# Routed experts' sums in the u buffers: more sets on the way, and the last x loaded beside the expert tiles

## The chip, the cores and the metric

The kernel runs on one core of a Trainium2 chip. The metric is the device time of one execution in microseconds (us), taken as the median of the runs shown. One further execution was taken with the hardware profiler on; all rows of profiles come from it.

## The reference

One decoder layer on x of shape (4, 512, 512) in f32: a selective state space block, a smooth-quantised gated linear block with weights that differ by batch, and a mixture of experts with top-2 routing over 16 experts and a shared expert. Each has a layernorm before it and a residual sum after it. The change is in the last part:

```python
routing = softmax(x @ gate_w.T)
topw, sel = top_k(routing, 2)
topw = topw / sum(topw)
hmid = silu(einsum('th,eih->tei', x, w1)) * einsum('th,eih->tei', x, w3)
moe_out = einsum('tei,ehi->th', hmid * combine[:, :, None], w2)   # combine: topw at sel
shared = sigmoid(x @ shared_gate_w.T) * (silu(x @ ws_gate.T) * (x @ ws_up.T) @ ws_down.T)
x = x + moe_out + shared
```

## The kernel before

The 2048 tokens are worked on in four batches of 512. Long scans over the state space fill the first 1450 us or so; behind them run, as Python generators, the back of each batch (`back`: output projection, quantised block, `moe_front` with the router and the shared expert) and the routed experts in two groups of two batches (`GROUPS`, `experts`). Group 0 is batches 0 and 1, group 1 is batches 2 and 3.

**Routed experts of a group.** `sort` puts the 1024 tokens x 2 choices in order of expert into 31 tiles of 128 rows; unused tiles have row numbers out of bounds, and their gathers move nothing. `expert_tiles` loads for each tile the tokens (`xs`, L1337, 256 KB) and the expert's weights (`wx`, L1146, 768 KB) by indirect DMA from POOL's queue. It then turns the tokens (PE L338, ACT L1357), multiplies (PE L1365), makes the gated product (ACT L1368, DVE L349 and L1371, tile `hs`), multiplies again (PE L1375), copies the result out (ACT L1378, `ys`, three buffers) and stores it to `y_d` in DRAM (SP, L1381). Up to three tiles are on their way at a time (`bank.depth`), and up to eight are loaded ahead (pool `last`, eight buffers).

**Sums of a group.** When the tiles are over, token block t (128 tokens, eight blocks to a group) has its sum made: x3 (residual plus shared expert) is loaded (SP, L1165), the two results of each token are gathered from `y_d` (POOL, L1168, two gathers), two DVE instructions add them with their weights into x (L1178), and SP stores the block to the output (L1185). I call what a block needs a set. `staged` writes the stages out as a software pipeline: in each step the later stages of earlier blocks come first, and an empty stage (`nothing`) puts one more set between load and add. Group 0 has its x in the tag `xs` and its two results in the tag `wx` of pool `experts`, with two buffers each; group 1 has them in the same tags of pool `last`, with eight.

**What sets the order of work.** Each engine, SP's and POOL's DMA queues among them, executes in the order in which the program was written. The class `Pace` carries a model of each engine's time and of the DMA queue (by tile name, it does not know that a buffer is used again), and the loop at the end of `run` (L1464) always advances the generator whose wait is over first in that model. So the model decides where on DVE a sum's add stands among the tiles' work. Group 0's sums start when group 1's first tiles have been loaded (`("begun", 1)`), group 1's when its tiles are over.

**The u buffers.** Pool `us` has 17 buffers of 128 x 512 f32. They hold `u`, the conv output of each batch (28 tiles in all go through them), until the batch's output projection is over; nothing uses them later.

Of the kernel before, what the change touches and what calls it, by code (L numbers as in the profile page):

```python
# [8 lines left out]
F32 = mybir.dt.float32  # L9
# [3 lines left out]
ALU = mybir.AluOpType  # L13
# [4 lines left out]
P = 128  # L18
B = 4
L = 512  # L20
DM = 512
# [39 lines left out]
class Bank:  # L61
# [21 lines left out]
    def staged(self, items, product, *stages, freed=1):  # L83

        gap = [nothing] * (self.depth - freed)
        return staged(items, product, *gap, *stages, every=1 if gap or self.depth == freed else freed, bank=self)
# [181 lines left out]
class Kernel:  # L268
# [860 lines left out]
    def experts(self, sb, group, bank, ahead):  # L1129


        nc = self.nc
        first, n = GROUPS[group]
        T, t0 = n * NT, first * NT
        NS = 2 * T + E - 1
        yield lambda: ("route", first + n - 1) in self.done
        place = lambda: (self.last, 8) if self.last else (sb, ahead)
        pos = sb.tile([P, T, 2], U32, name=f"pos{group}", bufs=1)
        tok = sb.tile([P, NS], U32, name=f"tok{group}", bufs=1)
        wrow = sb.tile([P, NS], U32, name=f"wrow{group}", bufs=1)  # L1140
        ws = {}

        def weights(s):

            ws[s] = place()[0].tile([P, W2 + DM], F32, name="wx")
            nc.gpsimd.indirect_dma_start(  # L1146
                out=ws[s],
                out_offset=None,
                in_=self.wexp,
                in_offset=bass.IndirectOffsetOnAxis(ap=wrow[:, s : s + 1], axis=0),  # L1150
                bounds_check=E * P - 1,
                oob_is_err=False,
            )

        yield from self.sort(sb, bank, group, pos, tok, wrow, lambda: [weights(s) for s in range(ahead)], min(ahead, 3))
        y_d = self.dram.tile([NS * P, DM], F32, name=f"y_d{group}")
        yield from self.expert_tiles(group, place, bank, NS, tok, ws, weights, self.xn_d[group], y_d)
        self.done.add(("tiles", group))

        yield lambda: ("moe", first + n - 1) in self.done and ("begun", len(GROUPS) - 1) in self.done  # L1160
        xr, ys = {}, {}

        def load(t):
            xr[t] = sb.tile([P, DM], F32, name="xr4", tag="xs")
            nc.sync.dma_start(xr[t], self.x3[t0 + t])  # L1165
            ys[t] = sb.tile([P, 2, DM], F32, name="yg", tag="wx")
            for i in range(2):
                nc.gpsimd.indirect_dma_start(  # L1168
                    out=ys[t][:, i, :],
                    out_offset=None,  # L1170
                    in_=y_d,
                    in_offset=bass.IndirectOffsetOnAxis(ap=pos[:, t, i : i + 1], axis=0),
                )
            return ys[t], xr[t]

        def add(t):
            for i in range(2):
                nc.vector.scalar_tensor_tensor(  # L1178
                    xr[t], ys[t][:, i, :], self.topw[:, t0 + t, i : i + 1], xr[t], ALU.mult, ALU.add
                )  # L1180
            return xr[t]

        def store(t):
            b, r = divmod(t0 + t, NT)
            nc.sync.dma_start(self.out[b, r * P : (r + 1) * P, :], xr[t])  # L1185

        yield from staged(range(T), load, *[nothing] * (ahead - 2), add, store)

    def sort(self, sb, G, group, pos, tok, wrow, first_weights, few):

# [136 lines left out]
        G.done(pk)  # L1327
        yield

    def expert_tiles(self, group, place, bank, NS, tok, ws, weights, xn_d, y_d):  # L1330

        nc = self.nc
        xs, rows = {}, xn_d.shape[0]

        def load(s):
            xs[s] = place()[0].tile([P, DM], F32, name="xs")
            nc.gpsimd.indirect_dma_start(  # L1337
                out=xs[s],
                out_offset=None,
                in_=xn_d,  # L1340
                in_offset=bass.IndirectOffsetOnAxis(ap=tok[:, s : s + 1], axis=0),
                bounds_check=rows - 1,
                oob_is_err=False,
            )
            if s not in ws:
                weights(s)

        def steps(s):

            sb, ahead = place()  # L1350
            few = min(ahead, 3)
            yield PE, xs[s], bank.free
            tp = bank.take([P, NK, P])
            self.transposes(tp, xs[s], NK)
            yield ACT, tp
            xT = sb.tile([P, NK, P], F32, name="xT", bufs=few)
            nc.scalar.copy(xT, tp)  # L1357
            bank.done(tp)
            w = ws[s]
            yield PE, xT, w, bank.free  # L1360
            ph = bank.take([P, 2, P])
            for i in range(2):
                for k in range(NK):
                    o = (2 * k + i) * P
                    nc.tensor.matmul(ph[:, i, :], w[:, o : o + P], xT[:, k, :], start=(k == 0), stop=(k == NK - 1))  # L1365
            yield ACT, ph
            h = sb.tile([P, P], F32, name="hs", bufs=few)
            nc.scalar.activation(h, ph[:, 0, :], AF.Tanh, scale=0.5)  # L1368
            yield h
            self.swish(h, h, ph[:, 0, :])  # L1370
            nc.vector.scalar_tensor_tensor(h, h, 0.5, ph[:, 1, :], ALU.mult, ALU.mult)  # L1371
            bank.done(ph)
            yield PE, h, bank.free
            py = bank.take([P, DM])
            nc.tensor.matmul(py, h, w[:, W2:], start=True, stop=True)  # L1375
            yield ACT, py
            y = sb.tile([P, DM], F32, name="ys", bufs=few)
            nc.scalar.copy(y, py)  # L1378
            bank.done(py)
            yield SP, y  # L1380
            nc.sync.dma_start(y_d[s * P : (s + 1) * P, :], y)  # L1381

        going = []
        loaded = started = ended = 0
        while ended < NS:
            while loaded < NS and loaded - ended < place()[1]:
                load(loaded)
                loaded += 1
            self.done.add(("begun", group))
            while started < loaded and len(going) < bank.depth:  # L1390
                going.append(Steps(self.pace, steps(started)))
                started += 1
            self.pace.update()
            one = min(going, key=lambda g: self.pace.ready(g.wait))
            yield one.wait
            one.go()
            if one.over:
                going.remove(one)
                ended += 1
# [231 lines left out]
```

## Time and profile before

| | us |
|---|---|
| median of 3 runs | 1704.43 (1701.28 to 1705.39) |
| profiled execution: time | 1707.47 |
| profiled execution: span | 1705.8 |
| last y_d store issued | 1673.9 |
| group 0's sums: first gather, last add | 1530.3, 1603.8 |
| group 1's sums: first gather, last add | 1676.7, 1702.1 |

How to read the lines below. PE is the matmul engine, PEld its weight load, DVE the vector engine, ACT the scalar engine, POOL GpSimd, SP the sync engine (its queue is SPq). A group of instructions shows line, engine, operation, output <- inputs, shapes, count | busy us, mean ns | idle us of that engine just before, and what ended most of it. A stage table has start:end, length, busy us of each engine with its number of instructions in brackets, the granted TensorE clock as a share of full speed, the busy share of the 16 DMA engines, and GB/s. Lines of the timeline have start, length, engine, line, operation, and in square brackets the idle time before it with what ended it.

### The profile page before, as it was taken

What the parts mean: (1) busy time and instruction counts of PE and PEld (TensorE: products, weight loads), DVE (VectorE), ACT (ScalarE), POOL (GpSimd) and SP (SyncE); (2) the same over time, 40 slices, a digit from 0 to 9 for tenths busy, and PEclk for the clock granted to TensorE, in tenths of its full rate; (3) what the DMA queues carried; (4) which work ended last, traced back from release to release, by engine and by line L of the source; (5) the groups of instructions that cost most, each with busy time, mean ns of one, the idle gap of its engine ahead of it and who ended that gap; (6) DMA issues with size and microseconds to landing.
All of it is one profiled execution on the core that took longest, in us unless ns stands there. A gap on an engine that the chain in (4) does not pass through costs nothing. (4 is left out here: it accounts for less than half of the span.)

```text
span 1705.8 us, 16157 instructions
## 1 busy us (share of the span) xinstructions
PE 1270.8 (75%) x4916; PEld 641.2 (38%) x4924; DVE 1230.2 (72%) x1367; ACT 912.4 (53%) x1490; POOL 1127.5 (66%) x911
## 2 busy tenths in 40 slices
PE   6768577659666687997669848766568989788891
PEld 2222122113332243434234314434243467545681
DVE  3286999997998798898889978888897643443213
ACT  3365677654778765556876522777653136401340
POOL 1175999886888797777879654788785532153443
PEclk9978689759798788999888978878878999789896
DMA  3464455574554465764456572546574653367846
GB/s 104 105 156 111 93 134 118 115 196 86 128 110 100 96 178 140 179 170 110 92 122 165 132 217 57 151 121 154 152 218 140 240 192 107 129 254 235 336 137 221
DMA packets 108310, 255.89 MB, mean 150 GB/s; under 512 B 16192, under 2 KB 20416, under 8 KB 108224
## 3 DMA queue, kind: packets, MB, share of 16 engines
q1 hardware_dynamic: 91776, 198.21, 45.1%
q0 software_dynamic: 16448, 56.65, 9.6%
q8 instruction: 39, 0.64, 0.2%
q14 instruction: 47, 0.39, 0.1%
HBM read 158.59 MB, written 45.88 MB: 120 GB/s over the span
## 5 line engine op out<-in xcount | busy, mean ns | idle before, releaser
L634 POOL TENSOR_TENSOR bu<-bc,rep 128x1024 f32<-128x1024 f32 x256 | 602.7, 2359 | 186.5 <-DVE da L641 155.8
L641 DVE TENSOR_TENSOR_SCAN da<-da,bu 128x1024 f32<-128x1024 f32 x256 | 585.9, 2289 | 73.3 <-POOL bu L634 52.7
L632 ACT ACTIVATE da<-rep,a_sb 128x512 f32<-128x512 f32 x512 | 353.0, 691 | 313.1 <-DVE h L647 288.6
L647 DVE TENSOR_TENSOR h<-da,bc 128x1024 f32<-128x1024 f32 x256 | 312.3, 1220 | 25.8 <-PE py L659 15.3
L659 PE MATMUL py<-h,sel 128*32 128x512 f32 x1024 | 168.7, 680 | 59.3 <-DVE h L647 59.3
L1146 POOL DMA_INDIRECT wx<-in_wexp,wrow x62 | 63.3, 1021 | 82.3 <-PE bank L1375 32.8
L392 PE MATMUL bank_a<-xnT,win 128*128 128x512 f32 x192 | 99.3, 665 | 15.3 <-DVE gz L349 8.3
L448 POOL TENSOR_TENSOR u<-u,tap 128x511 f32<-128x511 f32 (+2 forms) x72 | 91.3, 1268 | 16.4 <-ACT tap L444 14.1
L659 PEld LDWEIGHTS py<-h,sel 128*32 128x32 f32 x1024 | 30.6, 117 | 177.0 <-DVE h L647 93.9
L392 PE MATMUL bank_g<-xnT,win 128*128 128x512 f32 x168 | 83.4, 642 | 3.2 <-DVE gz L349 2.1
L603 POOL TENSOR_TENSOR sp_e<-sp_e,dd 128x512 f32<-128x512 f32 x32 | 40.6, 1270 | 62.7 <-ACT dd L598 62.7
L1337 POOL DMA_INDIRECT xs<-xn_d,tok x62 | 63.9, 1030 | 19.4 <-issue 13.7
L392 PE MATMUL bank_b<-xnT,win 128*128 128x512 f32 x120 | 62.7, 671 | 18.1 <-ACT sp_r L592 16.4
L392 PEld LDWEIGHTS bank_a<-xnT,win 128*128 128x128 f32 x192 | 40.2, 216 | 73.0 <-issue 52.0
L1168 POOL DMA_INDIRECT yg<-y_d,pos x32 | 32.2, 1005 | 48.9 <-DMA y_d<-ys 25.5
L1365 PE MATMUL bank<-xT,wx 128*128 128x128 f32 x448 | 55.4, 282 | 1.0 <-ACT xT L1357 1.0
L327 POOL TENSOR_SCALAR ln_scale<-ln_mv 128x1 f32<-128x1 f32 x48 | 11.1, 231 | 67.8 <-DVE ln_mv L320 64.6
L1178 DVE SCALAR_TENSOR_TENSOR xr<-yg,topw,xr 128x512 f32<-128x512 f32 x32 | 23.8, 754 | 43.2 <-DMA xr<-x 23.7
L1365 PEld LDWEIGHTS bank<-xT,wx 128*128 128x128 f32 x448 | 53.6, 197 | 3.4 <-issue 1.4
L711 PE MATMUL bank_a<-wout,u 128*128 128x512 f32 x92 | 45.4, 650 | 11.7 <-DMA wout<-in_wout 6.1
L392 PEld LDWEIGHTS bank_g<-xnT,win 128*128 128x128 f32 x168 | 33.3, 205 | 52.2 <-issue 43.7
L655 PE MATMUL py<-u,skip 128*128 128x512 f32 x64 | 37.8, 676 | 10.8 <-DVE u L681 10.8
(407 smaller groups left out, 2490.6 us busy)
## 6 DMA issues: line engine op xcount, KB each, us to landing
rep<-dd SPq DMA_DIRECT2D x128, 512.0 KB, 8.2
win<-in_win SPq DMA_DIRECT2D x64, 256.0 KB, 3.0
y_d<-ys SPq DMA_DIRECT2D x62, 256.0 KB, 2.5
x<-xr SPq DMA_DIRECT2D x48, 256.0 KB, 2.1
xr<-x SPq DMA_DIRECT2D x48, 256.0 KB, 4.4
bc<-rows_d SPq DMA_DIRECT2D x32, 256.0 KB, 5.4
gz_d<-gz SPq DMA_DIRECT2D x32, 256.0 KB, 3.0
gzl<-gz_d SPq DMA_DIRECT2D x32, 256.0 KB, 4.5
```

Source lines behind the costliest of these rows:

```text
L392: nc.tensor.matmul(pj, win[:, k, :], xnT[:, k, :], start=(k == 0), stop=(k == NK - 1))
L448: nc.gpsimd.tensor_add(u[:, j:], u[:, j:], v[j][:, j:])
L603: nc.gpsimd.tensor_sub(e, e, du)
L632: nc.scalar.activation(da[:, i, :], rep[:, i, 0, :], AF.Exp, scale=self.a_sb[:, q, g : g + 1])
L634: nc.gpsimd.tensor_mul(bu, st["bc"][0, g].unsqueeze(1).to_broadcast([P, NP, L]), rep[:, :, 1, :])
L641: self.nc.vector.tensor_tensor_scan(daf, daf, buf, 0.0, ALU.mult, ALU.add)
L647: self.nc.vector.tensor_mul(h, st["da"].pop((c, n)), st["bc"][1, g].unsqueeze(1).to_broadcast([P, NP, L]))
L659: nc.tensor.matmul(py[q * CH : (q + 1) * CH, :], self.sel, st["h"][c, g, q // NP][:, q % NP, :], start=False, stop=(g == NG - 1),)
L711: nc.tensor.matmul(po[t], st["u"][c][:, t * P : (t + 1) * P], wout[:, c, :], start=(c == part[0]), stop=(c == part[-1]),)
L1146: nc.gpsimd.indirect_dma_start(out=ws[s], out_offset=None, in_=self.wexp, in_offset=bass.IndirectOffsetOnAxis(ap=wrow[:, s : s + 1], axis= ...
L1337: nc.gpsimd.indirect_dma_start(out=xs[s], out_offset=None, in_=xn_d, in_offset=bass.IndirectOffsetOnAxis(ap=tok[:, s : s + 1], axis=0), bo ...
L1365: nc.tensor.matmul(ph[:, i, :], w[:, o : o + P], xT[:, k, :], start=(k == 0), stop=(k == NK - 1))
```

## The change

Group 0's sums take their x and their two results from the pool `us`, in tiles of one buffer each, so that three buffers make a set; and there are three empty stages instead of none, so that five sets are on the way. Group 1 keeps its results in pool `last` with six empty stages as before, but has its x in `us`. A new function `some`, called by `expert_tiles` when all 31 tiles' loads are written, loads the eight x of group 1's sums there, provided that group 0's sums and the last `moe_front` are already written.

```diff
+        xr = {}
+
+        def fetch(t):
+            xr[t] = self.us.tile([P, DM], F32, name="xr4", tag="u")
+            nc.sync.dma_start(xr[t], self.x3[t0 + t])
+
+        def some():
+
+            if sb is self.last and not xr and {("sums", 0), ("moe", B - 1)} <= self.done:
+                for t in range(T):
+                    fetch(t)
+
+        yield from self.expert_tiles(group, place, bank, NS, tok, ws, weights, some, self.xn_d[group], y_d)
...
         def load(t):
-            xr[t] = sb.tile([P, DM], F32, name="xr4", tag="xs")
-            nc.sync.dma_start(xr[t], self.x3[t0 + t])
-            ys[t] = sb.tile([P, 2, DM], F32, name="yg", tag="wx")
+            if t not in xr:
+                fetch(t)
+            if sb is self.last:
+                both = sb.tile([P, 2, DM], F32, name="yg", tag="wx")
+                ys[t] = [both[:, i, :] for i in range(2)]
+            else:
+                ys[t] = [self.us.tile([P, DM], F32, name="yg", tag="u") for i in range(2)]
...
-        yield from staged(range(T), load, *[nothing] * (ahead - 2), add, store)
+        yield from staged(range(T), load, *[nothing] * (6 if sb is self.last else 3), add, store)
+        self.done.add(("sums", group))
...
             self.done.add(("begun", group))
+            if loaded == NS:
+                some()
```

More of the change, by code (lines that the diff above doesn't have):

```diff
@@ L1156, in experts @@
         y_d = self.dram.tile([NS * P, DM], F32, name=f"y_d{group}")
-        yield from self.expert_tiles(group, place, bank, NS, tok, ws, weights, self.xn_d[group], y_d)
+        xr = {}
[7 more added lines that the diff above has]
+        yield from self.expert_tiles(group, place, bank, NS, tok, ws, weights, some, self.xn_d[group], y_d)
         self.done.add(("tiles", group))
         yield lambda: ("moe", first + n - 1) in self.done and ("begun", len(GROUPS) - 1) in self.done
-        xr, ys = {}, {}
+        ys = {}
         def load(t):
-            xr[t] = sb.tile([P, DM], F32, name="xr4", tag="xs")
-            nc.sync.dma_start(xr[t], self.x3[t0 + t])
-            ys[t] = sb.tile([P, 2, DM], F32, name="yg", tag="wx")
+            if t not in xr:
[5 more added lines that the diff above has]
+                ys[t] = [self.us.tile([P, DM], F32, name="yg", tag="u") for i in range(2)]
             for i in range(2):
                 nc.gpsimd.indirect_dma_start(
-                    out=ys[t][:, i, :],
+                    out=ys[t][i],
                     out_offset=None,
@@ L1173, in load @@
                 )
-            return ys[t], xr[t]
+            return *ys[t], xr[t]
         def add(t):
@@ L1178, in add @@
                 nc.vector.scalar_tensor_tensor(
-                    xr[t], ys[t][:, i, :], self.topw[:, t0 + t, i : i + 1], xr[t], ALU.mult, ALU.add
+                    xr[t], ys[t][i], self.topw[:, t0 + t, i : i + 1], xr[t], ALU.mult, ALU.add
                 )
@@ L1328, in sort, with expert_tiles @@
         yield
-    def expert_tiles(self, group, place, bank, NS, tok, ws, weights, xn_d, y_d):
+    def expert_tiles(self, group, place, bank, NS, tok, ws, weights, some, xn_d, y_d):
         nc = self.nc
```

## The prediction

> **What bounds the kernel now.** First the page: no engine is full over the span, so the edited stage has to be read by itself: adds of 754 ns that sat idle 43.2 us, 23.7 of them for x. The edited code runs only after about 1490 us.
>
> ```profile
> span 1705.8 us, 16157 instructions
> ...
> L1178 DVE SCALAR_TENSOR_TENSOR xr<-yg,topw,xr 128x512 f32<-128x512 f32 x32 | 23.8, 754 | 43.2 <-DMA xr<-x 23.7
> ```
>
> Next the stage table of the tail, cut at the starts of the transposes of each three tiles of group 1 (the bank depth is three). Columns: stretch, length, busy time of PE, PEld, DVE, ACT, POOL, granted clock, DMA share, GB/s.
>
> ```profile
> 1564.40:1583.00 18.60, 12.24 (x67) 8.75 (x66) 3.71 (x9) 3.57 (x8) 8.49 (x10) 0.75 0.86 313
> 1583.00:1592.78 9.78, 9.78 (x68) 8.19 (x67) 3.11 (x8) 4.16 (x9) 6.60 (x7) 0.96 0.98 365
> 1592.78:1607.07 14.29, 10.55 (x67) 8.00 (x66) 3.14 (x8) 3.47 (x8) 8.76 (x9) 0.90 1.03 410
> 1607.07:1620.60 13.53, 12.57 (x67) 10.69 (x66) 1.73 (x6) 4.65 (x10) 3.21 (x4) 0.72 0.72 292
> 1620.60:1630.01 9.41, 9.41 (x67) 7.79 (x66) 1.73 (x6) 4.06 (x9) 5.98 (x6) 1.00 0.87 279
> ```
>
> The last row is a round of three tiles bound by TensorE at full clock: 9.41 us, as are all later ones to tile 30. Tiles 4 to 15 took 18.60+9.78+14.29+13.53 = 56.2 us where four such rounds are 37.6: 18.6 us are lost here. The chain of waits says to what.
>
> ```profile
> 1560.48 6.90 DMA out<-xr
> 1567.40 8.09 DMA xr<-x
> 1575.61 0.76 DVE xr L1178
> ...
> 1577.72 5.50 PE bank L1375 x6
> ...
> 1584.32 10.40 DMA out<-xr
> 1594.73 8.17 DMA xr<-x
> 1603.03 0.76 DVE xr L1178
> ```
>
> The sums of group 0 have two x buffers. SP waits until a store of out has left one (6.90 us), only then loads x into it (8.09), and the add waiting for it stands on DVE ahead of the hs of tiles 4 to 6. PE then idles 6.36 us, and runs six L1375 matmuls in 5.5 us that take 2.74 in a warm round: the granted clock of that stage is 0.75. The same again before tile 12. In the list of waits from 1530 to 1610, that is (total us, times, longest)
>
> ```profile
> DVE xr L1178 <- DMA xr<-x: 23.7, 4, 10.3
> ...
> ACT ys L1378 <- DMA y_d<-ys: 8.4, 3, 4.9
> ...
> PE bank L1375 <- DVE hs L1371: 6.4, 1, 6.4
> ```
>
> and on SP's own queue (engine, line, what it waited for; us in total, times, longest)
>
> ```profile
> SPq L1165 <- DMA out<-xr: 31.1, 6, 9.7
> ```
>
> The end, last: POOL issues the 16 gathers of group 1 when the last y_d has landed.
>
> ```profile
> 1674.39 3.70 SPq L1165 DMA_DIRECT2D xr<-x  x8
> 1676.67 0.96 POOL L1168 DMA_INDIRECT yg<-y_d,pos  x1 [25.52 <-DMA y_d<-ys]
> ...
> 1697.09 0.95 POOL L1168 DMA_INDIRECT yg<-y_d,pos  x1 [0.30 <-issue]
> ...
> 1702.07 0.75 DVE L1178 SCALAR_TENSOR_TENSOR xr<-yg,topw,xr 128x512 f32<-128x512 f32 x1 [1.12 <-DMA yg<-y_d,pos]
> ```
>
> **The change, part by part.** No instruction is added: 16 x loads, 32 gathers, 32 adds, 16 stores as before. Their buffers and places move.
>
> *Five sets of group 0 on the way.* Sets 0 to 3 are loaded at once, set t+4 with the add of t. 28 tiles u have gone through the 17 buffers, so set t takes allocations 28+3t to 30+3t, and each waits for the one 17 before it. Sets 0 to 4 replace u's whose out_proj is long over: no wait. On SP two more x loads go ahead of L999 at 1491 (2 x 0.41 us): those land at 1496 and serve an add at 1551.73, so nothing. x4 follows at about 1495, x5 to x7 each directly behind the issue (no longer the landing) of the store of set 0, 1, 2, by the old add times 1541, 1545, 1554. On POOL, the gathers of sets 2 and 3 move up behind 1535.0 (4 x 1.26 us, to 1540), set 4 to about 1543; old times 1541 to 1555. They pass no tile gather: the ninth xs (1556.70) comes after, and wx of tile 9 waits for PE until 1559.69 anyway. DMA has room: the loads and outs that leave the crowd after 1559 are yg of sets 5 to 7 (1.57 MB), some x and outs, together 2.4 MB by my count; between 1540 and 1560 the share was 0.59.
>
> *A wait added.* The second gather of set 5, 6, 7 gets the buffer of x0, x1, x2, and so waits on POOL for the landing of that set's store. With adds 0 to 2 at about 1539, 1543, 1552 and 2 to 4 us for a store here, that is until 1545, 1548, 1557. Behind it on POOL stands the xs of tile 9, at most 2 us late; its weights are wanted at about 1575 and land 8.9 us after issue, so a hold is free until 1566. Before, POOL waited 12.9 us for adds in the same place.
>
> *What DVE then sees.* The adds wait only for loads four steps old: set 7 lands at about 1562, its add falls at about 1565. The adds (12 us in all) move ahead of tile 7, among the shared expert's DVE work of 1540 to 1567, where DVE is half idle. So the four waits of 23.7 us go, with both PE stalls and the cold rounds after them.
>
> *What is late next.* DMA. A round loads and stores 3 x (786+262+262) KB = 3.93 MB; the busiest stage above moved 410 GB/s, so 9.6 us. y_d landed after 8 to 11.6 us in the crowd, and only three ys buffers stand between ACT and it: a round shorter than the landing plus 0.7 us makes ACT wait (the 8.4 us above). I give each of the four rounds 0.7 us for this, 40.5 us in all, and 1.5 us for the two rounds of tiles 16 to 21, which become crowded. Gain 56.2 - 40.5 - 1.5 = 14.2 us; bounds 18.6 (no crowd) and 0 (see the rivals).
>
> Here a rule speaks against the change. The Trainium skill, "DMA: Bandwidth & Descriptors", section "Where 436 GB/s comes from", says that transfers between HBM and SBUF are held to some 358 GB/s per core. By the rule a round is 3.93 MB / 358 = 11.0 us, six rounds 66 instead of 62, and the gain about 10. The stage row with 410 (14 us long) is over the rule; I take the row.
>
> *x of the last sums.* Eight SP issues (3.7 us) move from 1674.4 to about the time when tile 24 is over, between y_d stores of a stage with a DMA share of 0.26 (rounds of tiles 25 to 30); their buffers are those of group 0's sets 2 to 4, free by then. SP is idle there, a y_d store slips by at most 3.7 us, ys has three buffers, nothing. At the end 2.1 MB (5 to 6 us of DMA) leave a stretch that POOL sets: 16 gathers at the usual 1.255 us start within 18.8 us, they took 20.4 (some 1.39 to 1.46 us each). I take this 1.6 us, and 0.6 of the last landing (5.0 us, against 3.7 in the lighter 1530 to 1559), 2.2 in all; bounds 0 and 4.
>
> **Sum.** 14.2 + 2.2 = 16.4 us of the profiled 1707.5 (span 1705.8) gives 1691; the profiled run is 3 us over the median 1704.4, so against that 1688.
>
> **The rivals.**
> *The crowd keeps the time (A).* With the stall gone TensorE asks for weights sooner, y_d lands after 11.6 us as in 1590 to 1600, and rounds are 12.3 us: six of them 74, against 56.2+18.8 = 75 before. Only the end's 2 us is left: 1702. For it: DMA shares of 0.98 and 1.03 now. Against: those rounds also carried group 0's sums, and the round at 0.98 took only 9.78. A half-way form, rounds of 11, gives 1694.
> *POOL held by the store's landing (B), the slower one.* If a store of set 0 to 2 stands on SP behind a y_d or x3 store that waits, the gather of set 5 to 7 holds POOL, and with it xs and wx of tile 9 on. From 1566 each us of hold is a us of PE; it must last to about 1582 to eat the gain and to 1590 to reach 1711. For it: SP is in order, and a store of out took up to 14.8 us to land. Against: the y_d stores start only at 1560, and adds 0 to 2 have nothing late before them.
> *The change doesn't bite (C).* If the written order still puts adds before their data, DVE waits as before, for the gathers: half of the 23.7 us stays, the gain is 7 + 2: 1695.
>
> **How the numbers follow.** Forecast 0.58 (1688, 1681 to 1693), half-way A and C 0.22 (1693 to 1699), full A 0.08 (1700 to 1705), B 0.12 (1710 to 1716). 0.3% is 5 us, about what a measurement of this kernel can tell from no change. Below 1699.3: 0.80; within: 0.08; above 1709.5: 0.12, as B when it acts is seldom small. The range goes from 1680 (both upper bounds, 22.6 us, and a us or two of noise) to 1702, leaving out B and some of A.
>
> **What would show it.** Right: no DVE wait for x at L1178 before 1650, SP's wait on out gone, tiles 4 to 15 in 38 to 43 us at a clock near 1.0, all adds of group 0 before about 1570, eight x loads among the y_d stores before 1660, 16 last gathers within 19 us. Wrong: a wait of POOL for out over 8 us, ACT ys waits for y_d over 2 us a round, PE idle behind wx, or DVE waiting for yg in front of an hs.

## The result, and the profile after

The changed kernel takes 1691.13 us (median of 7 runs, 1685.40 to 1695.48), the kernel before, beside it, 1704.22 us. The ratio is 0.9923, 95% interval 0.9905 to 0.9941: 13.1 us faster. (Beside the later experiments the kernel before has medians of 1703.55 to 1704.52 us; each ratio is to the runs beside it.) The forecast was 1688, with a range of 1680 to 1702. A repeat on another chip gave 1689.97 us and a ratio of 0.9924 (0.9901 to 0.9948).

The page of the profiled execution (1690.85 us) has this span. Lines in the changed kernel are numbered higher: the add L1178 is L1194, the x load L1165 is L1161, the store L1185 is L1201, the gather L1168 is L1184, and the tile lines L1365, L1375, L1381 are L1382, L1392, L1398.

```profile
span 1689.1 us, 16148 instructions
```

The stage table, cut as before at the first transposes of each three tiles (the last three columns are PE's clock, the share of the DMA engines and GB/s): tiles 4 to 21, and tiles 28 to 30 in the last row.

```profile
1563.30:1572.67 9.37, 9.37 (x67) 7.79 (x66) 2.47 (x7) 3.57 (x8) 3.50 (x4) 1.00 1.00 394
1572.67:1582.08 9.41, 9.41 (x68) 7.79 (x66) 1.72 (x6) 4.06 (x9) 5.97 (x6) 1.00 1.01 386
1582.08:1591.49 9.41, 9.41 (x67) 7.79 (x66) 1.72 (x6) 4.06 (x9) 4.98 (x5) 1.00 1.02 379
1591.49:1602.14 10.65, 9.52 (x68) 7.79 (x66) 1.72 (x6) 4.06 (x9) 6.98 (x7) 1.00 1.02 395
1602.14:1611.55 9.41, 9.41 (x68) 7.79 (x66) 1.72 (x6) 4.06 (x9) 5.97 (x6) 1.00 0.95 365
1611.55:1621.65 10.10, 9.51 (x68) 7.79 (x67) 1.72 (x6) 4.06 (x9) 5.98 (x6) 1.00 0.27 83
...
1640.47:1651.19 10.72, 9.51 (x68) 7.79 (x67) 1.73 (x6) 4.06 (x9) 0.00 (x0) 1.00 0.21 79
```

Four rounds that took 18.60, 9.78, 14.29 and 13.53 us now take 9.37, 9.41, 9.41 and 10.65, with the clock at 1.00 throughout, though the DMA engines are full for the first 38 us of it. PE is the bound in three of the four rounds, with no idle time, and DMA just keeps up.

The timeline of DVE shows where group 0's adds went. All sixteen are over at about 1560, with no idle time before any of them (a bracket would stand at the end of the line), and the hs of tiles 4 on waits for ACT alone:

```profile
1542.43 2.98 DVE L1194 SCALAR_TENSOR_TENSOR xr<-yg,topw,xr 128x512 f32<-128x512 f32 x4
...
1558.28 1.53 DVE L1194 SCALAR_TENSOR_TENSOR xr<-yg,topw,xr 128x512 f32<-128x512 f32 x2
...
1567.03 0.29 DVE L349 SCALAR_TENSOR_TENSOR hs<-hs,bank_g 128x128 f32<-128x128 f32 x1 [2.78 <-ACT hs L1385]
```

In the list of POOL's waits from 1500 on, a gather waits once for an older set's buffer, and it waits for an add, not for a store to land (total, times and longest in us):

```profile
POOL yg L1184 <- DVE xr L1194: 0.9, 1, 0.9
```

In the list of all engines from 1560 to 1660, two of ACT's waits at its copies into ys:

```profile
ACT ys L1395 <- PE bank_b L338: 1.5, 1, 1.5
...
ACT ys L1395 <- DMA y_d<-ys: 1.0, 1, 1.0
```

The second of these is in the round of 10.10 us. The first, in the round of 10.65 us, is put down to PE, but ACT's other copies of the kind waited 0.6 us for PE; that this one too waited for a ys buffer is an inference that the kernel with ys in u, below, tests. A third such wait is in the round of tiles 28 to 30, behind the eight early x loads, and it too is put down to PE (timelines of SP and of ACT):

```profile
1631.77 3.67 SPq L1161 DMA_DIRECT2D xr<-x  x8
1635.54 22.22 SPq L1398 DMA_DIRECT2D y_d<-ys  x8
...
1642.02 0.59 ACT L1395 COPY ys<-bank 128x512 f32<-128x512 f32 x1 [1.58 <-PE bank_a L338]
```

The end stage did not become shorter. The last y_d store is issued at 1657.44 and the span ends at 1689.1: 31.7 us, against 31.9 before. In the timeline of its POOL and DVE:

```profile
1660.20 0.95 POOL L1184 DMA_INDIRECT yg<-y_d,pos  x1 [26.83 <-DMA y_d<-ys]
...
1663.58 0.75 DVE L1194 SCALAR_TENSOR_TENSOR xr<-yg,topw,xr 128x512 f32<-128x512 f32 x1 [8.02 <-DMA yg<-y_d,pos]
1663.97 1.18 POOL L1184 DMA_INDIRECT yg<-y_d,pos  x1 [0.30 <-issue]
...
1668.12 0.75 DVE L1194 SCALAR_TENSOR_TENSOR xr<-yg,topw,xr 128x512 f32<-128x512 f32 x1 [0.93 <-DMA yg<-y_d,pos]
1668.32 1.37 POOL L1184 DMA_INDIRECT yg<-y_d,pos  x1 [0.30 <-issue]
1669.99 0.94 POOL L1184 DMA_INDIRECT yg<-y_d,pos  x1 [0.30 <-issue]
1670.01 0.75 DVE L1194 SCALAR_TENSOR_TENSOR xr<-yg,topw,xr 128x512 f32<-128x512 f32 x1 [1.13 <-DMA yg<-y_d,pos]
...
1680.88 1.47 POOL L1184 DMA_INDIRECT yg<-y_d,pos  x1 [0.30 <-issue]
```

The gathers are still spread over 20.7 us (1660.20 to 1680.88), and seven of the sixteen take 1.07 to 1.47 us instead of 0.95. Each of those seven starts at least 0.10 us into an add; the one at 1669.99 starts just before its add and is not slow, and one that starts 0.03 us into an add (1671.24) is not slow either. That became a theory of its own, below.

**How the later tables are made.** The long scans are the same in all kernels, and still tile 4 starts up to 7 us apart from one profiled execution to the next. So profiles are compared from the tail's own marks: the rounds of three tiles, from the transposes of tile 4 to the issue of the last y_d store ("tiles"), and from there to the end of the span ("end"). Before: tiles 109.5, end 31.9. After: tiles 94.1, end 31.7. Each is one execution. A second one of the changed kernel has 93.8 and 32.2, so its stages repeat within about half a us. Those of kernels that stall can differ more: the kernel with early x only, below, leaves group 0's sums as they were, and its tiles take 107.1 where the kernel before has 109.5.

### The profile page after: what moved, and what is told of

Its sections match the earlier page's. It is cut to its first block, busy times and chain, and to the rows that moved or that the text cites. A ratio compares the mean times of both kernels' runs of the same rounds, so it can differ in the third digit from the quotient of the medians.

```text
span 1689.1 us, 16148 instructions
## 1 busy us (share of the span) xinstructions
PE 1271.8 (75%) x4924; PEld 640.6 (38%) x4924; DVE 1229.9 (73%) x1367; ACT 912.7 (54%) x1490; POOL 1129.1 (67%) x911
## 5 line engine op out<-in xcount | busy, mean ns | idle before, releaser
L659 PE MATMUL py<-h,sel 128*32 128x512 f32 x1024 | 173.1, 701 | 55.1 <-DVE h L647 55.0
L659 PEld LDWEIGHTS py<-h,sel 128*32 128x32 f32 x1024 | 31.9, 120 | 176.4 <-DVE h L647 90.0
L1354 POOL DMA_INDIRECT xs<-xn_d,tok x62 | 64.0, 1032 | 19.4 <-issue 13.1
L1184 POOL DMA_INDIRECT yg<-y_d,pos x32 | 33.3, 1042 | 36.8 <-DMA y_d<-ys 26.8
L327 POOL TENSOR_SCALAR ln_scale<-ln_mv 128x1 f32<-128x1 f32 x48 | 11.1, 230 | 67.4 <-DVE ln_mv L320 64.2
L1382 PE MATMUL bank<-xT,wx 128*128 128x128 f32 x448 | 53.6, 276 | 1.7 <-ACT xT L1374 1.7
L1382 PEld LDWEIGHTS bank<-xT,wx 128*128 128x128 f32 x448 | 51.8, 192 | 4.2 <-ACT xT L1374 2.2
L349 DVE SCALAR_TENSOR_TENSOR hs<-hs,bank 128x128 f32<-128x128 f32 x28 | 8.0, 285 | 53.9 <-ACT hs L1385 53.9
```

The source lines that it names most:

```text
L659: nc.tensor.matmul(py[q * CH : (q + 1) * CH, :], self.sel, st["h"][c, g, q // NP][:, q % NP, :], start=False, stop=(g == NG - 1),)
L1354: nc.gpsimd.indirect_dma_start(out=xs[s], out_offset=None, in_=xn_d, in_offset=bass.IndirectOffsetOnAxis(ap=tok[:, s : s + 1], axis=0), bo ...
```

## The experiments

Theory 1 was that of the prediction: group 0's adds stood on DVE waiting for x, which waited on SP for a buffer. What had to be told apart was the buffer from the lead (how early a set is loaded), and this half of the change from the other (x of the last sums loaded early).

| kernel | ratio to before (95%) | tiles us | rounds of tiles 4-6, 7-9, ... 28-30 | end us |
|---|---|---|---|---|
| before | 1 | 109.5 | 18.60 9.78 14.29 13.53 9.41 9.41 9.41 9.41 9.41 | 31.9 |
| changed | 0.9923 (0.9905 to 0.9941) | 94.1 | 9.37 9.41 9.41 10.65 9.41 10.10 9.41 9.41 10.72 | 31.7 |
| changed, once more | 0.9924 (0.9901 to 0.9948) | 93.8 | 9.37 9.41 9.41 9.87 9.57 10.34 9.41 9.41 10.74 | 32.2 |
| five sets, late x | 0.9914 (0.9889 to 0.9938) | 92.7 | 9.37 9.41 9.41 9.80 9.62 10.63 9.41 9.41 9.41 | 32.1 |
| early x only | 1.0013 (1.0002 to 1.0024) | 107.1 | 16.05 11.38 14.53 9.86 10.12 9.41 9.41 9.41 10.72 | 32.2 |
| two sets in u | 0.9958 (0.9938 to 0.9977) | 97.8 | 9.47 9.41 13.47 9.41 9.41 10.53 9.41 9.41 11.02 | 31.4 |
| only group 0's x in u | 0.9950 (0.9930 to 0.9970) | 98.8 | 9.79 10.24 11.16 10.68 13.00 9.41 9.41 9.41 9.41 | 31.0 |
| changed, x in PSUM at the end | 0.9931 (0.9913 to 0.9948) | 94.3 | 9.37 9.41 9.41 10.65 9.40 9.81 9.41 9.41 11.22 | 30.3 |
| changed, x one by one | 0.9923 (0.9905 to 0.9941) | 93.0 | 9.37 9.41 9.41 11.05 9.41 9.88 9.41 9.41 9.41 | 32.7 |
| changed, ys in u | 0.9901 (0.9882 to 0.9920) | 90.9 | 9.38 9.41 9.40 9.38 9.37 9.38 9.37 9.37 9.65 | 32.1 |
| all three | 0.9894 (0.9876 to 0.9913) | 90.6 | 9.37 9.41 9.41 9.37 9.37 9.38 9.37 9.37 9.38 | 29.8 |

### One half of the change and the other

The changed kernel without the early x:

```diff
-            if loaded == NS:
-                some()
```

> The changed kernel without `some`: group 0 with five sets in u buffers, but the last sums' eight x are loaded at the end, behind the last y_d store, as before. Theory 1 (all of the gain is the wait of group 0's adds for x that is gone; the end stage took 31.9 us before and 31.7 after): as the changed kernel, 1690 to 1693 us, and an end stage of 31 to 33 us from the issue of the last y_d store. Rival (the early x saves the predicted 2 us at the end, hidden in the spread): 1693 or more, an end stage of 33.5 us or more.

1686.38 us, a little under what was expected. All of the gain is there; the end is 32.1 us, not 33.5, and the round of tiles 28 to 30, 10.72 us with early x, is at 9.41. So the second half brings nothing, and costs 1.3 us in that round of the profile. The ratio is lower than that of the changed kernel (0.9914 against 0.9923), but the intervals overlap, so the times alone do not show the loss.

The other half alone (group 0 as before, the last x early). The cut is against the kernel before; `fetch`, `some` and its call are added as in the change:

```diff
...
-            xr[t] = sb.tile([P, DM], F32, name="xr4", tag="xs")
-            nc.sync.dma_start(xr[t], self.x3[t0 + t])
+            if t not in xr:
+                xr[t] = sb.tile([P, DM], F32, name="xr4", tag="xs")
+                nc.sync.dma_start(xr[t], self.x3[t0 + t])
...
```

> The second half alone: the last sums' x in u buffers and loaded beside the tiles; group 0's sums with two sets and their old buffers. Theory 1: no gain, 1703 to 1705 us, with the DVE waits for x of 20 us or more as before. Rival (early x is worth the predicted 2 us): 1701 to 1702.5 us.

1705.78 us: no gain, if anything a loss (ratio 1.0013, interval above 1). In the list of waits DVE still waits for x:

```profile
DVE xr L1192 <- DMA xr<-x: 23.6, 4, 10.8
```

The slow round of 10.72 us at the end of the tiles is there too, so it goes with the early x. The profiled execution was one of this kernel's faster ones: its tail is 2.0 us shorter than that of the kernel before, and the medians say otherwise. Its rounds of tiles 4 to 15 take 51.8 us where the kernel before has 56.2, with the same stall in them; a difference of this size between single profiles of such kernels tells nothing.

### The buffer or the lead

The changed kernel with two sets of group 0 on the way:

```diff
-        yield from staged(range(T), load, *[nothing] * (6 if sb is self.last else 3), add, store)
+        yield from staged(range(T), load, *[nothing] * (6 if sb is self.last else 0), add, store)
```

> The changed kernel with no empty stage for group 0: two sets on the way as before, but each in fresh u buffers, so that neither x nor results wait for an older set to leave. Theory 1a (the reuse of a buffer is what cost): most of the gain stays, 1691 to 1695 us, DVE waits at the adds under 5 us. Theory 1b (the lead of a set is what counts: x of set t+1 is still issued on SP behind the store of set t-1, and lands late in the crowd): half or less of the gain, 1697 to 1703 us, DVE still waits 10 us or more at the adds.

1694.97 us, just over half of the gain in time; in the profile 11.7 of the 15.4 us of tiles (109.5 to 97.8). Neither expectation holds as it stood: the time is in the range of 1a, the waits of DVE at the adds are 6.1 us (3.8 for yg, 2.3 for x) where 1a had under 5 and 1b 10 or more, and PE hardly feels them (the round of tiles 4 to 6 takes 9.47 us). What is left is the one round of 13.47 us, and its lines in the timeline of ACT and PE name another cause:

```profile
1577.77 0.59 ACT L1395 COPY ys<-bank 128x512 f32<-128x512 f32 x1 [1.60 <-DMA y_d<-ys]
...
1579.73 0.58 ACT L1395 COPY ys<-bank 128x512 f32<-128x512 f32 x1 [1.37 <-DMA y_d<-ys]
...
1580.85 3.68 PE L1382 MATMUL bank_b<-xT,wx 128*128 128x128 f32 x16 [2.33 <-ACT xT L1374]
```

ACT waits twice for a ys buffer to reach DRAM, the next xT stands behind that, PE idles 2.33 us and runs 16 matmuls in 3.68 us (granted clock 0.54) where a round at full clock has 1.95. 2.33 and 1.73 are the 4.06 us that the round lost. So the lead matters, but through ys, not through a wait at an add: the three y_d stores of tiles 4 to 6, whose buffers these copies need, took 8.5 to 11.1 us to land here, and 4.5 to 7.8 in the changed kernel. In this kernel the last set's two gathers and x load, and the last three stores of out, fall between 1554 and 1565, among the tiles' weights; with five sets the gathers and x loads are issued by 1548. That this late traffic is what holds the y_d stores is likely, but no run tests it alone.

Only group 0's x in u buffers, everything else as before:

```diff
-            xr[t] = sb.tile([P, DM], F32, name="xr4", tag="xs")
+            if sb is self.last:
+                xr[t] = sb.tile([P, DM], F32, name="xr4", tag="xs")
+            else:
+                xr[t] = self.us.tile([P, DM], F32, name="xr4", tag="u")
```

> The kernel before with one edit: group 0's x in u buffers. Results, two sets on the way, and the last sums as before. Theory 1a: SP's wait for the landing of out (31.1 us) goes and with it most of the 23.7 us of DVE; 1692 to 1697 us. Theory 1b (lead counts, and the results' two buffers hold POOL): 1698 to 1704 us, with the DVE waits now on x or yg in the crowd.

1694.12 us, as 1a expected: about two thirds of the gain by the ratios, and 10.7 of the 15.4 us of tiles. Freeing x from the store of its predecessor is the largest single part. SP no longer waits for out, and DVE's wait for x is down from 23.7 us to 7.2 in one piece. What is left, in rounds of 10 to 13 us, is for the most part ACT waiting for ys again (5.2 us in five waits). That the results' two buffers cost anything by themselves is not shown: the kernel above has the results in u too, and it is no faster (0.9958 against 0.9950, intervals overlapping, though it also carries the early x).

### Why the end stayed as long

Theory L: a gather that starts while a DVE add with two operands in SBUF runs is held until the add is nearly over. The profile after gives the amounts. With 0.95 us as the gather alone, and each add 0.75 us long, the time left in the add at the gather's start is 0.36, 0.36, 0.25, 0.55, 0.63, 0.51 and 0.65 us for the seven slow ones, and they are 0.23, 0.24, 0.12, 0.42, 0.50, 0.38 and 0.52 us too long: always 0.12 to 0.13 us less. The first six add up to 1.9 us, which is 20.7 against the 18.8 that the gathers need alone. To test it, x goes to PSUM, so that an add has one operand in SBUF:

```diff
...
+            if sb is self.last:
+                px[t] = bank.take([P, DM])
+                nc.scalar.copy(px[t], xr[t])
+                return *ys[t], px[t]
...
+            x = px.get(t, xr[t])
             for i in range(2):
                 nc.vector.scalar_tensor_tensor(
-                    xr[t], ys[t][i], self.topw[:, t0 + t, i : i + 1], xr[t], ALU.mult, ALU.add
+                    x if i == 0 else xr[t], ys[t][i], self.topw[:, t0 + t, i : i + 1], x, ALU.mult, ALU.add
                 )
...
```

> The changed kernel, but at the end ACT copies each early x into a PSUM bank, and the two adds of a block read the results from SBUF and x from PSUM (the second writes to SBUF for the store). Theory L (a gather that starts while a DVE add with two SBUF operands runs is held until the add ends: the slow gathers of the end stage are those, and moving x could not help them): the 16 gathers all take under 1.0 us and start within 18.9 us instead of 20.7, the end stage is 29.5 to 30.5 us instead of 31.7, the time 1 to 2 us under the changed kernel's. Rival D (DMA crowding slows them): gathers as before, 20 us or more, end stage 31 to 32 us.

In its timeline every gather takes 0.94 to 0.96 us, also the six that start 0.25 to 0.63 us into such an add, where a hold would show. Three of these, and the last gather:

```profile
1661.84 0.75 DVE L1199 SCALAR_TENSOR_TENSOR bank<-yg,topw,bank 128x512 f32<-128x512 f32 x1 [8.17 <-DMA yg<-y_d,pos]
1662.09 0.95 POOL L1184 DMA_INDIRECT yg<-y_d,pos  x1 [0.30 <-DMA yg<-y_d,pos]
...
1667.80 0.76 DVE L1199 SCALAR_TENSOR_TENSOR bank<-yg,topw,bank 128x512 f32<-128x512 f32 x1 [1.15 <-DMA yg<-y_d,pos]
1668.34 0.95 POOL L1184 DMA_INDIRECT yg<-y_d,pos  x1 [0.30 <-issue]
...
1670.59 0.75 DVE L1199 SCALAR_TENSOR_TENSOR xr<-yg,topw,bank 128x512 f32<-128x512 f32 x1 [2.03 <-DMA yg<-y_d,pos]
1670.84 0.95 POOL L1184 DMA_INDIRECT yg<-y_d,pos  x1 [0.30 <-issue]
...
1677.09 0.95 POOL L1184 DMA_INDIRECT yg<-y_d,pos  x1 [0.30 <-issue]
```

They start within 18.8 us (1658.31 to 1677.09), and the end is 30.3 us, where the kernels whose adds have both operands in SBUF end in 31.0 to 32.7. The gain of 1.4 us is in the profile; in time the kernel (1690.55 us) cannot be told from the changed one.

The adds of group 1 left out altogether:

```diff
-            for i in range(2):
+            for i in range(0 if sb is self.last else 2):
```

> The changed kernel without the adds of group 1's sums: the blocks of batches 2 and 3 are stored without their routed part; gathers and stores stay, and the stores now crowd in at the start of the gathers. Theory L: with no DVE work beside them no gather takes over 1.0 us, and they start within 18.9 us. Rival D: several still take 1.1 to 1.5 us, 20 us or more in all.

Its time, of a single execution, is 1686.86 us. All sixteen gathers take 0.94 to 0.96 us and start within 18.8 us, while the eight stores and the gathers move the same bytes, the stores sooner. So it is the adds, not the crowd on the DMA engines. The Trainium skill ("GPSIMD Engine Reference", section "1. Specifications") has the rule: POOL shares its SBUF interfaces with VectorE, and contends with DVE instructions that have two SBUF inputs. The runs agree for the issue of an indirect DMA, which the adds held by up to 0.52 us each here.

### What is left in the tiles

The early x one with each of the last tiles, instead of eight in a row:

```diff
...
-                for t in range(T):
-                    fetch(t)
+                while len(xr) < min(T, ended + 8 - NS + 1):
+                    fetch(len(xr))
...
```

> The changed kernel, with the eight early x loaded one with each of the last tiles instead of all at once. Theory S (eight loads in a row stand on SP in front of a y_d store, and ACT waits for a ys buffer: the round of tiles 28 to 30 took 10.7 us where it takes 9.4 with late x): that round is back at 9.4 to 9.6 us, the time about 1 us under the changed kernel's, as with late x. Rival (the slow round comes from something else in the changed order): it stays at 10.5 us or more.

The round of tiles 28 to 30 is back at 9.41 us, as theory S has it. The y_d stores of the last rounds land after at most 3.7 us here; with eight loads in a row the first store behind them takes 6.3 to 6.9 us, in the five other kernels whose traces tell its landing. The time is not lower (1692.23 us): in the profiled execution the round of tiles 13 to 15 was 11.05 us and the end 32.7.

The ys of group 1 from its tenth tile on in u buffers, which rotate over 17 instead of three:

```diff
-            y = sb.tile([P, DM], F32, name="ys", bufs=few)
+            if xn_d is self.xn_d[1] and s >= 9:
+                y = self.us.tile([P, DM], F32, name="ys", tag="u")
+            else:
+                y = sb.tile([P, DM], F32, name="ys", bufs=few)
```

> The changed kernel, with the ys of group 1 from its tenth tile on in u buffers instead of three of their own. Theory Y (what is left of the loss in tiles 4 to 30 is ACT waiting for y_d to leave one of three ys buffers): every round of three from tile 13 to 30 takes 9.4 to 9.5 us, the stretch from tile 4 to the last y_d store 91 to 92 us instead of 94.1, the time 2 to 3 us less. Rival (DMA itself sets the pace, a round moves 3.93 MB): the waits turn up at xs or wx on PE, and the stretch stays within 1 us of 94.1.

1686.72 us. Every round from tile 4 to 27 is at 9.37 to 9.41 us, the last at 9.65; tiles take 90.9 us, 3.3 less. PE does not wait for xs or wx. The slow rounds of the changed kernel were ACT waiting for ys. The intervals of the two ratios overlap, so this gain too is one of the profile.

### All three together

> The changed kernel with what the experiments point to: ys of group 1 from its tenth tile on in u buffers, the early x one with each of the last tiles, and x in PSUM for the last adds. Worked out from the profiles: 94.1 us from tile 4 to the last y_d store become 91, the end stage of 31.7 becomes 30.2, so 4 to 5 us under the changed kernel: 1684 to 1687 us, ratio to the kernel before 0.988 to 0.990. Rival (the parts take from each other, for instance the x copies on ACT or the x loads in the way of y_d): 1688 us or more.

> The changed kernel once more, on the same chip and beside the same runs of the kernel before as the version with all three: 1688 to 1693 us, ratio 0.991 to 0.994.

1684.15 us against 1689.97 for the changed kernel beside it: tiles 90.6, end 29.8, no gather over 1 us. That is 5.8 us of medians, with intervals of the ratios that still touch (0.9876 to 0.9913, and 0.9901 to 0.9948), and 20 us under the kernel before. The kernel with ys in u alone has 0.9901, with an interval of 0.9882 to 0.9920, so the times do not show that the other two parts add anything to it.

## Why the prediction was right, point by point

- *The four waits of 23.7 us go, with the PE stalls and the cold rounds.* Right. The main term was 14.2 us; the profiles have 15.4 (109.5 to 94.1), with a few us of spread in the first of these, as the kernel with early x only shows. Tiles 4 to 15 take 38.8 us where 40.5 were forecast, and tiles 16 to 21 19.5 where 20.3 were. The allowance of 0.7 us a round for y_d landing late was a little high: one round paid 1.24 us, three nothing.
- *The wait added on POOL.* This step was wrong, and by luck the sum did not depend on it, since the hold was taken as free. No gather waited for a store of out. The stores of sets 0 to 2 were issued at 1539.90, 1543.99 and 1545.44 and landed 3.9, 4.4 and 4.7 us later, but the second gathers of sets 5 to 7 had started before that, at 1541.64, 1545.09 and 1547.79. So these gathers did not have the buffers of x0 to x2, as the count of 17 allocations back says; which rule gives out the buffers is not shown. POOL's one wait was 0.9 us, for an add. Rival B had nothing to act on.
- *All adds before about 1570.* Right, 1560. The adds of sets 0 to 2 came at 1538.3 to 1545.4, earlier than forecast (set 2 at 1552). Rival C, adds written ahead of their data, did not happen: no DVE wait for x or yg before 1650.
- *What is late next is DMA, and ACT at ys.* Right as the mechanism of what is left, as the kernel with ys in u shows; rival A, that it would keep all of the time, was wrong: with 1.00 to 1.02 of the DMA engines busy over 38 us, PE lost only 1.2 us. Here the row was the right choice over the rule that was weighed: rounds moved 379 to 395 GB/s for 38 us, above 358. (The working has a slip there: its own six rounds are 40.5 + 20.3 = 60.8 us, not 62, and by the rule the gain of the rounds is 9, not 10.)
- *The eight SP issues slip a y_d store by at most 3.7 us, ys has three buffers, nothing.* This step failed, though the slip was sized well: the y_d store came at 1635.54, some 3.6 us late. What was left out is its landing behind the eight loads, 6.3 to 6.9 us where the kernels with late x have 2 to 2.5. ACT, one buffer short, waited 1.58 us, PE was behind ACT, and the round of tiles 28 to 30 lost 1.3 us (10.72 against 9.41).
- *The end gains 2.2 us.* This step failed too: 0.2, and nothing in the second profile (32.2). The 1.6 us of slow gathers were put down to the crowd of x loads, and they come from the adds. With x there early the first add came 6.1 us after the last y_d store instead of 9.3, so more adds ran beside gathers: seven slow gathers instead of four. Of the 0.6 us for the last landing 0.4 came, and the gathers took 0.3 longer (20.4 to 20.7). Over all kernels whose adds have both operands in SBUF the gathers start within 19.3 to 20.4 us with late x, and 20.0 to 21.2 with early x.

The sum came out near the profile because two misses cancelled in part: 15.4 + 0.2 = 15.6 against 16.4. (The profiled executions are 16.6 us apart; 1.1 us of that lies ahead of tile 4.) The medians are 13.1 us apart, 3.5 us less than the profiles: the profiled execution of the kernel before took 1707.47 us, 3.25 over the median of its seven runs, and that of the changed kernel was 0.28 under its own. What made the one slower is not known.

## What to carry to other kernels

A tile that is loaded into, added to and stored from one buffer ties a load to the landing of an older store, and on an engine that runs in order its late user holds work that has nothing to do with it: giving only that tile more buffers brought two thirds of the gain here. When a transfer is moved to save time on a stage, first ask what sets that stage; here POOL's issue did, not the bytes, and the moved issues stood in front of a store that someone needed. Where POOL gathers beside DVE, a DVE operand in PSUM kept the two apart here, for 1.4 us of a profile and no difference in time that could be told.

## What the runs showed of the hardware

- A gather's issue on POOL takes 0.95 us here. In the end stages of the nine traces whose adds have both operands in SBUF (eight kernels), all 51 gathers that start 0.10 to 0.59 us into an add of 0.75 us are held until 0.12 to 0.13 us before its end; the 17 that start less than 0.10 us into one, or in its last 0.14 us, are not. With one operand in PSUM none is (sixteen of sixteen at 0.94 to 0.96 us).
- The DMA engines moved 379 to 395 GB/s between DRAM and SBUF, both ways together, over four rounds (38 us), with the granted clock at 1.00 beside them.
- After a PE pause of 2.33 us the next 16 matmuls took 3.68 instead of 1.95 us, at a granted clock of 0.54 (two sets in u), and after one of 1.86 us the next 48 took 7.25 us at 0.76 (only group 0's x in u). After one of 1.70 us (x in PSUM) the clock stayed at 1.00.
